# Expert tiles without gaps: 96 slots an expert instead of 128, in a two-block hybrid model on one core

## The chip, the cores and the metric

The kernel runs on one core of a Trainium2 chip. The metric is the device time of one execution in microseconds (us), and the lower the better. A core has TensorE (PE in the profile: matmuls, with its weight loads listed apart as PEld), VectorE (DVE), ScalarE (ACT), GpSimd (POOL) and SyncE (SP, which only issues transfers). Matmul results land in PSUM, of which a core has eight banks of 128 x 512 floats; everything else on the chip lies in SBUF.

## The reference, cut to what matters

1,024 tokens of 256 floats pass through two blocks. Every line below is applied to a layer-normed x and added to x.

```
x += shift-mix(x)              # block 0: a linear recurrence over time
x += first_ffn(x)              # 8 experts 256 -> 256, the best one of each token
x += state_space(x)
x += first_ffn(x)
x += attention_a(x)            # block 1: 16 heads of 16, 4 key groups, causal
x += second_ffn(x)             # 32 experts 256 -> 96 -> 256, the best four of each token
x += attention_b(x)            # the same shape, with a slope per head
x += second_ffn(x)

first_ffn:  p = softmax(x @ wg);  e = argmax p;  p[e] * (x @ W[e].T + b[e])
second_ffn: p = softmax(x @ router); the best 4, rescaled to sum 1;
            sum over them of w[e] * (silu(x @ gate[e].T) * (x @ up[e].T)) @ down[e].T
```

All of it is float32. In the inputs of this case, an expert gets at most 88 of a group's 512 tokens in the first FFN and at most 91 of them in the second (counted in the reference).

## The kernel before

The tokens are cut into two groups of 512 (g = 0, 1), and each group into four tiles of 128 tokens. Every stage is written for one group as a set of small generators, "streams", each of which yields after every few instructions. The name of a stream says what it is: A0 and A1 are shift-mix, F and G the first FFN in its two places, S state space, a and b the two attentions, e and f the second FFN after each, the digit the group, and a last letter the step. A list written out in the code, `ORDER`, names the streams one by one, and `follow` advances them in that order; so the order of instructions on each engine is fixed by this list. A second list, `BANKS`, gives the PSUM bank of every PSUM tile in the order in which the tiles are asked for. Stages of the two groups are woven together: e0 (second FFN of group 0) with attention a of group 1, attention b of group 0 with e1, f0 with attention b of group 1. Only f1 stands alone at the end.

**An expert FFN** (`second_ffn`, line 984; `first_ffn`, line 374, in the same manner) works by slots. `route` (990) computes the four experts of each token and its rank within each of them; its slot is `CAP * expert + rank`, with `CAP` = 128 (line 30). `send` (1042) scatters the normed tokens to these rows of a table `sent` in HBM, 16 indirect transfers a group on POOL's queue. Then 16 pairs of experts follow, two tiles of 128 rows a pair:

- `fetch` (1070): 256 rows from `sent` into `xe`, on SP's queue
- `turn` (1076): four TensorE transposes of 128x128 into a bank (`px`), ScalarE copies them to `xT`
- `gate` (1089): for each of the two tiles, two products (256 deep, so two halves of 128, line 198) of the 128 turned rows with 192 columns of gate and up weights, into `pgu`; ScalarE's silu, VectorE's product
- `turn_back` (1103): two transposes `ph`, VectorE copies `hT`
- `down` (1113): for each tile one product, 96 deep, with 256 columns, into `py`; VectorE copies it to `ye`; SP writes 256 rows of `done`

`back` (1129) gathers the rows of `done` with 16 indirect transfers on POOL's queue, and `add` (1141) adds each, weighted, to x. The first FFN has 8 experts, so 4 pairs; its `work` (491) is one product of 256 columns a tile and half, and VectorE adds a bias that lies in SBUF for all partitions (loaded in one transfer, line 1301). If any expert of any group had more than `CAP` tokens, a branch at the end (line 1516) computes all anew without slots.

**An attention** (`attention`, 774) holds its heads in strips of 32 partitions: partition 32 s + d holds depth d (of 16, and 16 helper rows) of key group s. A group's four units of 128 queries (batch b, query tile qt) go through five steps. `peaks` (842) makes scores to find the largest of each row: the keys were expanded before (`kb`, lines 801 to 806: four copies of the keys, each zero outside one strip), so a product takes 64 partitions, and two of them, on partitions 0 to 63 and 64 to 127, fill two banks; VectorE reduces each bank (line 864). `below` (870) turns the negated maxima and adds them to the queries (`qm`). `weights` (883) makes the transposed scores with the maxima taken off, again two products of 64 partitions at a time in two banks, and ScalarE's exp brings them to SBUF (`pT`, line 901), with the diagonal cut on POOL (904). `products` (909) multiplies them by the values: four products whose results have 32 partitions each, side by side in one bank (line 915). `finish` (921) divides and projects.

A float32 matmul appears in the trace as two weight loads and two matmul records, one after the other; a transpose as one of each.

## Time and profile before

| | |
|---|---|
| median of 14 runs | 739.22 us (734.62 to 742.86) |
| the profiled execution | 741.2 us |
| its span in the profile | 739.4 us |
| mean granted TensorE clock | 0.928 of full speed |
| TensorE busy | 630.8 us (85%), 3168 matmul records |
| VectorE busy | 489.7 us (66%) |
| GpSimd busy | 285.5 us (39%) |
| ScalarE busy | 258.1 us (35%) |
| moved by transfers | 94.01 MB |

A line of a group, as the profile writes it, has the line number in the code, the engine, the operation, what it writes and reads (names of tiles), the tile's shape as partitions x elements, and how often it occurs. For TensorE, a shape such as 64\*128 tells the rows and columns of the array that the matmul uses: 64 deep, and 128 partitions of result. A line of a timeline has a start, the time from there to the end of the last of its instructions, and the instructions; as matmuls are pipelined, the distance from one start to the next tells more of what an instruction costs than its own duration. A busy share is a share of time in which at least one instruction of the engine was under way. A table of stretches gives, for each, its length, the busy us and the number of instructions of PE, PEld, DVE, ACT and POOL, then the clock that TensorE was granted, the share of the DMA engines and the GB/s.

### The profile page before, as it was taken

Reading aid. Unit: us, or ns where it says so; the run is one execution under the profiler, and the core shown is the slowest. Engines: PE = TensorE matmul, PEld = TensorE weight load, DVE = VectorE, ACT = ScalarE, POOL = GpSimd, SP = SyncE. Lnnn points to the kernel's source line nnn. Section 1 sums busy time; section 2 is a strip of 40 time slices with the busy share of each in tenths; the row PEclk is TensorE's granted clock in tenths of the full one; section 3 lists DMA queues with packets and bytes.
Section 4 is the critical chain, followed back from the end, with each engine's and each line's share of the span. In section 5 each row is a group of like instructions: output and inputs, shape, how many; then the busy total and the mean of one; then the engine's idle time right before and its main releaser. Section 6 shows DMA issues by size and latency. Waiting matters only on the chain. (4 is left out here: it accounts for less than half of the span.)

```text
span 739.4 us, 10048 instructions
## 1 busy us (share of the span) xinstructions
PE 630.8 (85%) x3168; PEld 428.6 (58%) x3168; DVE 489.7 (66%) x1507; ACT 258.1 (35%) x476; POOL 285.5 (39%) x333
## 2 busy tenths in 40 slices
PE   4765859799999699998899998999996999999820
PEld 2343645366668455444369998853454449999810
DVE  7988536798854667758738546678867747645542
ACT  3522214667452122532354222332431345232200
POOL 3016233433642622511840726306704640625334
PEclk9896969999969699999999999999997999999965
DMA  6702333500004723690233867313100123877733
GB/s 194 263 0 72 139 118 128 182 0 1 1 28 156 268 74 107 216 318 15 86 100 129 271 218 245 122 58 100 44 1 22 65 86 111 267 229 207 226 113 104
DMA packets 70827, 94.01 MB, mean 127 GB/s; under 512 B 6896, under 2 KB 60656, under 8 KB 70128
## 3 DMA queue, kind: packets, MB, share of 16 engines
q1 hardware_dynamic: 62944, 72.31, 30.2%
q0 software_dynamic: 7680, 20.98, 9.1%
q8 instruction: 27, 0.44, 0.3%
q14 instruction: 32, 0.26, 0.1%
q10 hardware_dynamic: 144, 0.01, 0.0%
HBM read 50.29 MB, written 42.99 MB: 126 GB/s over the span
## 5 line engine op out<-in xcount | busy, mean ns | idle before, releaser
L1134 POOL DMA_INDIRECT yb_f<-done,bk_f x64 | 64.9, 1014 | 77.1 <-issue 23.7
L198 PE MATMUL pgu_f<-gu,xT_f 128*128 128x192 f32 x512 | 94.4, 331 | 0.0
L198 PEld LDWEIGHTS pgu_f<-gu,xT_f 128*128 128x128 f32 x512 | 85.2, 193 | 2.4 <-ACT xT_f L1086 0.8
L1046 POOL DMA_INDIRECT sent<-xn_f,to_f x64 | 62.7, 980 | 60.5 <-DVE to_f L1034 19.3
L1118 PE MATMUL py_f<-dw,hT_f 96*128 96x256 f32 x256 | 65.2, 382 | 0.6 <-DVE hT_f L1110 0.5
L1122 DVE COPY ye_f<-py_f 128x512 f32<-128x512 f32 x64 | 43.7, 686 | 24.6 <-PE py_f L1118 11.3
L864 DVE CUSTOM_DVE_ANT_0 junk_b<-pS_b,tri 128x128 f32<-128x128 f32 (+1 forms) x128 | 45.7, 357 | 17.0 <-PE pS_b L851 10.0
L864 DVE CUSTOM_DVE_ANT_0 junk_a<-pS_a,tri 128x128 f32<-128x128 f32 (+1 forms) x128 | 45.7, 357 | 13.5 <-PE pS_a L851 6.6
L1086 ACT COPY xT_f<-px_f 128x512 f32<-128x512 f32 x64 | 36.8, 587 | 40.0 <-PE px_f L1082 37.8
L1118 PEld LDWEIGHTS py_f<-dw,hT_f 96*128 96x128 f32 x256 | 44.7, 190 | 6.5 <-DVE hT_f L1110 1.4
L1098 ACT ACTIVATE he_f<-pgu_f 128x192 f32<-128x192 f32 x64 | 21.1, 331 | 77.8 <-PE pgu_f L198 68.4
L1144 DVE SCALAR_TENSOR_TENSOR x<-yb_f,wt_f,x 128x256 f32<-128x256 f32 x64 | 31.8, 503 | 21.2 <-DMA yb_f<-done,bk_f 20.7
L904 POOL TENSOR_SCALAR_AFFINE_SELECT pT_b<-pT_b 128x512 f32<-128x512 f32 x32 | 20.7, 672 | 47.2 <-ACT pT_b L901 47.0
L1100 DVE TENSOR_TENSOR he_f<-he_f,pgu_f 128x192 f32<-128x192 f32 x64 | 21.9, 348 | 25.3 <-ACT he_f L1098 25.0
L901 ACT ACTIVATE pT_a<-pST_a 128x512 f32<-128x512 f32 x48 | 25.6, 605 | 36.6 <-PE pST_a L893 36.0
L1082 PE MATMUL px_f<-ident,xe_f 128*128 128x128 f32 x256 | 36.6, 274 | 2.1 <-DMA xe_f<-sent 2.1
L1110 DVE COPY hT_f<-ph_f 96x256 f32<-96x256 f32 x64 | 26.1, 415 | 18.1 <-PE ph_f L1107 17.4
L901 ACT ACTIVATE pT_b<-pST_b 128x512 f32<-128x512 f32 x48 | 25.6, 600 | 33.0 <-PE pST_b L893 32.3
L904 POOL TENSOR_SCALAR_AFFINE_SELECT pT_a<-pT_a 128x512 f32<-128x512 f32 x32 | 19.9, 646 | 44.5 <-ACT pT_a L901 44.5
L1082 PEld LDWEIGHTS px_f<-ident,xe_f 128*128 128x128 f32 x256 | 30.4, 141 | 6.2 <-DVE x L1144 2.2
L198 PE MATMUL py_f<-W,xT_f 128*128 128x256 f32 x128 | 33.5, 413 | 0.2 <-ACT xT_f L488 0.2
L602 DVE SCALAR_TENSOR_TENSOR cv<-pcv,cw,cv 128x506 f32<-128x506 f32 (+5 forms) x36 | 26.3, 737 | 6.5 <-ACT cv L597 5.9
(298 smaller groups left out, 1328.3 us busy)
## 6 DMA issues: line engine op xcount, KB each, us to landing
xe_f<-sent SPq DMA_DIRECT2D x64, 256.0 KB, 3.2
done<-ye_f SPq DMA_DIRECT2D x64, 256.0 KB, 2.7
sent<-nil SPq DMA_DIRECT2D x16, 512.0 KB, 6.3
xe_f<-fsent SPq DMA_DIRECT2D x16, 256.0 KB, 2.9
fdone<-ye_f SPq DMA_DIRECT2D x16, 256.0 KB, 2.2
gu<-in_L1f_gate SPq DMA_DIRECT2D x4, 768.0 KB, 16.6
gu<-in_L1f_up SPq DMA_DIRECT2D x4, 768.0 KB, 11.9
dw<-in_L1f_down SPq DMA_DIRECT2D x4, 768.0 KB, 17.5
```

The source lines that it names most:

```text
L198: nc.tensor.matmul(dst, w(c), rhs(c), start=(c == 0), stop=(c == n - 1))
L602: nc.vector.scalar_tensor_tensor(cv[:, :, sh:], pcv[:, :, :S - sh], cw[:m, j, k:k + 1], cv[:, :, sh:], ALU.mult, ALU.add)
L864: nc.vector.tensor_tensor_reduce(out=junk[:, :w], in0=both[r][:, at:at + w], in1=tri[:, S - w:], scale=1.0, scalar=NEG, op0=ALU.add, op1=A ...
L901: nc.scalar.activation(pT.rearrange("p c q -> p (c q)"), pS, AF.Exp)
L904: nc.gpsimd.affine_select(pT, pT, pattern=[[0, AG], [1, P]], compare_op=ALU.is_ge, fill=zero, base=0, channel_multiplier=-1)
L1046: nc.gpsimd.indirect_dma_start(out=sent_to[g][t * TOPK + j], out_offset=bass.IndirectOffsetOnAxis(ap=to[:, t, j:j + 1], axis=0), in_=xn[:, ...
L1082: nc.tensor.transpose(px[:, j * P:(j + 1) * P], xe[q][:, k, c * P:(c + 1) * P], ident)
L1086: nc.scalar.copy(xT[q].rearrange("p k c t -> p (k c t)"), px)
L1118: nc.tensor.matmul(py[:, k * D:(k + 1) * D], hT[q][:, k, :], dw[:, 2 * q + k, :], start=True, stop=True)
L1122: nc.vector.tensor_copy(ye.rearrange("p k d -> p (k d)"), py)
L1134: nc.gpsimd.indirect_dma_start(out=yb, out_offset=None, in_=done[g], in_offset=bass.IndirectOffsetOnAxis(ap=kept_["back"][:, t, j:j + 1], ...
L1144: nc.vector.scalar_tensor_tensor(x[g][:, t, :], due[t, j], kept_["wt"][:, t, j:j + 1], x[g][:, t, :], ALU.mult, ALU.add)
```

## The change

Three things change, and the two lists are written anew for them.

1. `CAP` is 96. The table of an FFN has 96 rows an expert, so 3,072 rows instead of 4,096 in the second FFN and 768 instead of 1,024 in the first, and these rows are still cut into tiles of 128: 12 pairs of tiles instead of 16, and 3 instead of 4. A tile now holds rows of two experts, and the products with weights are made for pieces of it: `pieces` cuts a tile at the borders between experts into pieces of 64 or 32 rows that start at a multiple of their size. The result of a piece goes to the piece's own partitions.
2. The bias of the first FFN lies in SBUF by slots instead of by experts, in 12 transfers instead of one; the branch at the end loads it again for itself.
3. The expanded keys `kb` are gone. `peaks` and `weights` use the keys in their own strips of 32 partitions, four products at a time, into four banks.

```diff
-CAP = 128
+CAP = 96
-ORDER = """
...
+ORDER = """
...
-BANKS = """
...
+BANKS = """
...
+    def pieces(i):
+        at = 0
+        while at < P:
+            e, used = divmod(i * P + at, CAP)
+            n = next(n for n in (P, P // 2, P // 4)
+                     if n <= min(CAP - used, P - at) and at % n == 0)
+            yield e, slice(at, at + n)
+            at += n
...
+        pairs = E0 * CAP // (2 * P)
...
                 for j in range(2):
-                    e = 2 * q + j
-                    project(py[:, j * D:(j + 1) * D], lambda c: xT[q][:, j, c, :],
-                            lambda c: W[:, c, e * D:(e + 1) * D])
+                    for e, at in pieces(2 * q + j):
+                        project(py[at, j * D:(j + 1) * D], lambda c: xT[q][:, j, c, at],
+                                lambda c: W[:, c, e * D:(e + 1) * D])
...
-            kb = kept_["kb"] = pools["act"].tile([P, AG, TG], F32, tag="kb", name=f"kb_{name}", bufs=1)
-            for c in range(AG):
...
                 for c0 in range(0, 4, per):
-                    both = [bank("sq", f"pS_{n_}_{c0}_{r}") for r in range(2)]
+                    four = [bank("sq", f"pS_{n_}_{c0}_{s}") for s in range(AG)]
                     for c in range(c0, c0 + per):
-                        for r in range(2):
-                            rows, at = slice(64 * r, 64 * r + 64), (c - c0) * 2 * w
+                        for s in range(AG):
+                            rows, at = slice(32 * s, 32 * s + 32), (c - c0) * w
                             nc.tensor.matmul(
-                                both[r][:, at:at + 2 * w].rearrange("p (s k) -> p s k", s=2),
-                                qT[rows, c, q0:q0 + P],
-                                kb[rows, 2 * r:2 * r + 2, b * S:b * S + w],
-                                start=True, stop=True)
+                                four[s][:, at:at + w], qT[rows, c, q0:q0 + P],
+                                kT[rows, b * S:b * S + w], start=True, stop=True)
...
-                    for s0 in range(2):
-                        pairs = [(s, bank("st", f"pST_{n_}_{kt}_{s}")) for s in (s0, s0 + 2)]
-                        for s, pS in pairs:
-                            rows = slice(64 * (s // 2), 64 * (s // 2) + 64)
-                            nc.tensor.matmul(pS, kb[rows, s, k0:k0 + P],
+                    four = [bank("st", f"pST_{n_}_{kt}_{s}") for s in range(AG)]
+                    for s, pS in enumerate(four):
+                        rows = slice(32 * s, 32 * s + 32)
+                        nc.tensor.matmul(pS, kT[rows, k0:k0 + P],
...
-        pairs = E1 // 2
+        pairs = E1 * CAP // (2 * P)
...
                 for k in range(2):
-                    project(pgu[:, k, :], lambda c: xT[q][:, k, c, :],
-                            lambda c: gu[:, c, :, 2 * q + k, :])
+                    for e, at in pieces(2 * q + k):
+                        project(pgu[at, k, :], lambda c: xT[q][:, k, c, at],
+                                lambda c: gu[:, c, :, e, :])
...
                 for k in range(2):
-                    nc.tensor.matmul(py[:, k * D:(k + 1) * D], hT[q][:, k, :],
-                                     dw[:, 2 * q + k, :], start=True, stop=True)
+                    for e, at in pieces(2 * q + k):
+                        nc.tensor.matmul(py[at, k * D:(k + 1) * D], hT[q][:, k, at],
+                                         dw[:, e, :], start=True, stop=True)
...
-            nc.sync.dma_start(
-                bias, a["L0f_b"].rearrange("e d -> (e d)").partition_broadcast(P))
+            for i in range(E0 * CAP // P):
+                for e in range(i * P // CAP, ((i + 1) * P - 1) // CAP + 1):
+                    lo, hi = max(e * CAP - i * P, 0), min((e + 1) * CAP - i * P, P)
+                    nc.sync.dma_start(
+                        bias[lo:hi, i, :], a["L0f_b"][e, :].partition_broadcast(hi - lo))
```

The pieces repeat every three tiles (four experts). By width, in the order of the products: 64, 32, 32; then 64, 64; then 32, 32, 64.

## The prediction

> **What bounds the kernel now.** I read first the shares of the whole span, then a table of stretches, then two stretches of TensorE's timeline. The chain of waits at the page's end covers only the last gathers and says nothing of the middle.
>
> ```profile
> span 739.4 us, 10048 instructions
> PE 630.8 (85%) x3168; PEld 428.6 (58%) x3168; DVE 489.7 (66%) x1507; ACT 258.1 (35%) x476; POOL 285.5 (39%) x333
> ```
>
> The stretches show where the 85% lie:
>
> ```profile
> 290.00:380.00 90.00, 82.66 (x435) 39.89 (x435) 61.86 (x276) 36.28 (x72) 43.68 (x55) 1.00 0.48 152
> 380.00:460.00 80.00, 77.54 (x487) 70.98 (x482) 44.69 (x123) 27.86 (x59) 30.41 (x31) 0.98 0.63 199
> 460.00:570.00 110.00, 101.47 (x511) 61.06 (x511) 84.51 (x314) 36.71 (x70) 42.09 (x46) 0.96 0.20 61
> 570.00:640.00 70.00, 68.61 (x396) 45.24 (x393) 44.34 (x173) 28.82 (x56) 29.00 (x35) 0.99 0.36 112
> 640.00:708.00 68.00, 64.52 (x396) 58.77 (x395) 37.39 (x91) 18.15 (x42) 25.30 (x26) 1.00 0.71 223
> 708.00:740.00 32.00, 0.00 (x0) 0.00 (x0) 9.96 (x21) 0.00 (x0) 15.95 (x16) 0.51 0.36 104
> ```
>
> From 290 to 708 TensorE works 92 to 98% of the time, and no other engine comes near. These are the stretches that the change touches, so I count TensorE's time. The last 32 us (POOL's 16 gathers and their adds) and the first 100 (61 us of TensorE, chains of other engines) are left as they are.
>
> **What a matmul record costs** is read from one start to the next.
>
> ```profile
> 396.37 1.47 PE L198 MATMUL pgu_f<-gu,xT_f 128*128 128x192 f32 x8
> 397.67 0.38 PE L1107 MATMUL ph_f<-ident,he_f 128*96 128x128 f32 x2
> 397.89 0.60 PE L1082 MATMUL px_f<-ident,xe_f 128*128 128x128 f32 x4
> 398.33 1.03 PE L1118 MATMUL py_f<-dw,hT_f 96*128 96x256 f32 x4
> 399.22 1.57 PE L198 MATMUL pgu_f<-gu,xT_f 128*128 128x192 f32 x8
> ```
>
> 1.30 us for 8 records of 192 columns are 0.163 each; a transpose costs 0.109, a record of 256 columns 0.216 (median distance), one of 512 columns 0.429. A product is two records. Now the same where the shape of the used array changes:
>
> ```profile
> 306.30 1.13 PE L851 MATMUL pS_a<-kb_a,qT_a 64*128 64x256 f32 x8
> 307.37 1.13 PE L198 MATMUL po_a<-woa,cT_a 128*128 128x256 f32 x4
> 308.33 0.60 PE L248 MATMUL pt_a<-ident,xn_a 128*128 128x128 f32 x4
> 308.86 1.07 PE L915 MATMUL pctx_a<-pT_a,vaug 128*32 128x512 f32 x8
> 309.86 1.98 PE L198 MATMUL pk_a<-xnT_a,wka 128*128 128x512 f32 x4
> 311.77 1.13 PE L893 MATMUL pST_a<-qm_a,kb_a 64*128 64x512 f32 x4
> ```
>
> Two things are to be seen. Strips run side by side: the 8 records of 512 columns in four 32-wide strips (L915) take 1.00 us, where one after another they would take 3.43; so does each pair of 64-deep strips. And a change of shape costs time: the four transposes at 308.33 would end their issue at 308.77, the strips start at 308.86, 0.09 later; pk takes 1.91 for records worth 1.72. I compared the changes of shape in the whole trace: for each of the eight kinds that occur, the median of this gap is 0.092 to 0.096 us, whichever two shapes it joins. The first weights then load uncovered: 0.105 us more for 128 columns, 0.053 for 64 (the conv's 64-wide products: 0.481 to the second record, 0.429 after), 0.027 for 32. So a change costs 0.20 into full width or row strips, 0.15 into 64-wide, 0.12 into 32-wide columns.
>
> **Part by part, TensorE's time.** Two pieces of one width that follow each other lie in different strips: I call them one run. Three pairs of tiles (8 experts) have nine runs: 64 | 32 32 | 64 64, then 32 32 | 64 64 | 32 32, then 64 64 | 32 32 | 64. Neighbouring runs differ in width, so I take them as one after another, and the pieces of a run as side by side, as in L915.
>
> - `gate`: a piece is four records, a run 0.652 us. 48 pairs x 3 runs = 144 runs, 93.9 us; before, 64 pairs x 8 records = 83.5. **+10.4**
> - `down`: a run is 2 x 0.216. 144 runs, 62.2; before 256 records, 55.3. **+6.9**
> - the first FFN's `work`: a run is 4 x 0.216. 36 runs, 31.1; before 128 records, 27.6. **+3.5**
> - transposes: 16 pairs fewer x 6, and 4 pairs fewer x 4, at 0.109. **-12.2**
> - scores: `peaks` had 48 groups of two strips, each 0.86 us (two records of 512 or four of 256 deep in each strip); it has 24 groups of four strips, each again 0.86. `weights` likewise 48 to 24. **-41.2**. Four row strips aren't in the trace; two are (at full rate) and four column strips are. If four ran no faster than two, nothing of the 41 would be gained.
> - changes of shape, counted in the order of the built program: before 140 (112 into full width or row strips, 4 into 64-wide, 24 into 32-wide), 25.9 us; after 492 (153, 173, 166), 76.5. **+50.6**. 240 of the 492 lie between 64- and 32-wide pieces, the rest mostly around each pair's pieces, which transposes enclose.
>
> The sum is **+18.0 us**. [...]
>
> **Where the rows leave room.** (1) In `gate` and `work` the second piece stands behind four records of the first (each with its weight load). In the trace (pST groups that follow each other) a weight load passes at most three held instructions of the other strip; here it must pass five. If it can't, the second piece starts one record late: 7 of 9 runs, 16 x 7 x 0.163 + 4 x 7 x 0.216 = +24.3. `down` has two records a piece, the pattern of L915. Nearest is the rows' full overlap, so I take 0 and keep 24. [...] (2) A score group needs four free banks instead of two. Each is freed by an exp (0.60 us) or by reductions (0.29 to 0.42 each); a wait of one exp in each of 48 groups is +29, none if other products stand before it, as they do in the list; I take 0. (3) SP gets 12 bias transfers instead of one, at some 0.45 us of issue each, eight of them between the second and third fetch of F0. That is up to 4 us, in a stretch that TensorE doesn't fill; three pairs instead of four save about as much. I take 0.
>
> **Beside it, at nothing.** VectorE loses 16 x (348+415+686) ns, 4 x 0.69 and 8 x 0.484 (kb): 30 us. ScalarE loses 16 x (587+331) ns, 4 x 0.586 and 8 x 0.711: 23 us. About 13 of 94 MB aren't moved. TensorE covers all that, except where VectorE is nearly as full: 340 to 360 (17.2 of 20 us) and 500 to 540. There the shorter scores leave VectorE's reductions, unchanged in number, as the next bound, and TensorE gains only as far as the list has expert products to put there: both signs, some 10 us. TensorE's own idle time between 100 and 708 is 39 us, so a better list can't give more than that.
>
> **Rivals.**
> - *No drain between 64 and 32 wide*: then a tile's two or three pieces run side by side. gate takes 62.6, down 41.5, work 20.7: 41.6 less than before instead of 20.8 more; and 240 changes cost nothing, -32.4. Sum -76.8, so 662; with the late second piece 686. For it: strips work on their own, as L915 shows. Against: every pair of shapes in the trace drains. It decides the sign once a quarter of it holds (18 of 95).
> - *Pieces one after another*: 16 x 7 x (0.652+0.432) + 4 x 7 x 0.864 = +146, so 903. Against it is L915.
> - *Late second piece*: 781.
> - *The branch at the end is taken*: at most 91 tokens stand against 96 slots, so no. Its second FFN's products alone would add 32 x 4 x (8 x 0.429 + 8 x 0.216) = 660 us.
>
> **How the numbers follow.** The profiled execution took 741.2 us, 1.8 beyond its span and 2.0 above the median of 739.2. +18.0 gives 759.2 in its terms and **757** against the median. Chances: full overlap with drains 0.47 (own range 735 to 782), late second piece 0.26, no drain 0.15, one after another 0.05, and 0.07 for waits for banks or VectorE beyond the rest. The range of 80% goes from 686 (no drain, late piece) to 800 (late piece and part of the bank waits). Faster by over 0.3% (what a measurement can tell from no change): 0.15, a sixth of the first case, and little else: 0.25. Within it 0.05, slower 0.70.
>
> **What would show it.** In the profile after: gaps of 0.09 us and an uncovered load at each border of 64- and 32-wide records; a run of two gate pieces in 0.65 us (0.82 if late, 1.30 if one after another); score groups of 0.86 us plus a change; the stretch of f1, alone at the end, longer by some 17 us (4.3 for the runs; a quarter of the second FFN's 213 changes between widths at 0.135, and 24 blocks of pieces entered at 0.14 and left at 0.20, so 15.4; -2.6 for transposes). If 64- and 32-wide records start within 0.02 us of each other, the first rival holds. If VectorE passes TensorE where scores are made, the sum of TensorE alone was the wrong one.

## The result, and the profile after

The changed kernel takes **804.75 us** (median of 10 runs, 801.12 to 810.02) where the kernel before takes 739.88 (47 runs): 1.0893 times as long, interval 1.0863 to 1.0922. The sign was forecast, the size not: 757 with a range to 800. The profiled execution took 805.87 us. Its page, first the span and the first engine line:

```profile
span 804.2 us, 11830 instructions
...
PE 682.5 (85%) x4208; PEld 376.6 (47%) x4208; DVE 459.6 (57%) x1446; ACT 232.7 (29%) x429; POOL 281.0 (35%) x333
```

TensorE is busy for 52 us more with a third more records; VectorE lost the 30 us that were forecast, ScalarE 25. By busy time alone this looks like the kernel before, only longer. It isn't: where the scores are made there is less for TensorE to stream than before, and it takes longer. Here are 43 us among the scores of the first attention, in the table of stretches, before and then after (the columns from the second on: length, then busy us and instructions of TensorE, weight loads, VectorE, ScalarE and POOL, then the granted clock):

```profile
328.00:352.00 24.00, 19.47 (x115) 10.76 (x111) 20.42 (x91) 5.06 (x10) 4.00 (x6) 1.00 0.25 79
352.00:371.00 19.00, 16.37 (x91) 7.50 (x91) 14.35 (x74) 7.49 (x15) 15.43 (x18) 1.00 0.26 91
```

```profile
328.00:352.00 24.00, 16.57 (x85) 11.83 (x83) 15.03 (x62) 3.92 (x8) 3.63 (x5) 0.60 0.15 46
352.00:371.00 19.00, 19.00 (x75) 9.76 (x75) 13.62 (x59) 4.28 (x8) 11.06 (x12) 0.50 0.17 70
```

In the second row of after TensorE is busy for all of 19 us, with 75 records, at half clock; before, it ran 91 records in the same time and had time to spare. A busy share of 100% is here the sign of a slow clock, not of much work.

To say where the 65 us are I cut the main part into four stretches and each stretch into three kinds of time, worked out from the records of the two traces: a record streams its columns at the rate of 512 in 0.429 us, twice as long where the granted clock is half (in e16_clock, below, 46 records take 19 us at full clock and 47 take 39 us at half); records side by side count once. "Streaming" is this time at full clock, "half clock" what the slow clock adds to it, "nothing" the rest, in which TensorE streams no column (changes of shape, loads that nothing covers, waits). Scores 1 runs from the first score to the first gate product, e to e1's last gate product, scores 2 to f0's first, f to f1's last.

| us, before -> after | length | streaming | half clock | nothing |
|---|---|---|---|---|
| scores 1 | 117.6 -> 131.1 | 93.0 -> 78.8 | 0 -> 16.5 | 24.5 -> 35.8 |
| scores 2 | 115.7 -> 130.4 | 85.2 -> 81.7 | 2.7 -> 12.3 | 27.8 -> 36.4 |
| e | 108.6 -> 121.2 | 98.8 -> 91.3 | 1.7 -> 2.6 | 8.1 -> 27.3 |
| f | 96.0 -> 120.7 | 88.8 -> 91.7 | 0 -> 2.7 | 7.2 -> 26.3 |

So there are two losses. The stretches of expert products take 37 us more, nearly all of it "nothing": 312 changes of shape more (4 -> 157 and 0 -> 159) for 38.3 us, 0.12 each. The score stretches take 28 us more, though TensorE streams 18 us less there: 26 us of half clock and 20 us of "nothing" were added. The second loss is the one that was not forecast.

One border moved between the two kernels, and it shifts the shares. Before, 36 records of attention b's first queries, keys and scores (16 of 512 columns, 4 of 512, 16 of 256 in pairs of strips: 10.3 us of streaming at the rate above) stand ahead of e1's last gate product, so in row e; after, they stand behind it, in row scores 2. Like for like the expert stretches lost some 48 us and the score stretches some 18, in which TensorE streams 28 us less.

What TensorE waits for in the first score stretch, in the view of waits (total us, times, longest), before and then after:

```profile
PE pST_a L893 <- DVE qm_a L878: 3.5, 3, 2.3
PE pr_f L1013 <- DVE up_f L1008: 1.8, 1, 1.8
PE pm_a L874 <- DVE nmx L864: 1.2, 2, 0.9
PE po_a L198 <- ACT cT_a L946: 0.5, 1, 0.5
PE pcT_a L942 <- DVE cx_a L935: 0.3, 1, 0.3
```

```profile
PE pr_f L1005 <- DVE up_f L1000: 3.6, 1, 3.6
PE pcT_a L934 <- DVE cx_a L927: 2.2, 1, 2.2
PE po_a L190 <- ACT cT_a L938: 2.1, 3, 1.1
PE pST_a L885 <- DVE qm_a L872: 1.6, 2, 0.9
```

These are chains: scores, maxima on VectorE, turned maxima, queries less maxima, scores again, exp, context, division. TensorE waits longer for `up`, `cx` and `cT` than before, and less for `qm`; all waits of this view together grow from 7.7 to 15.2 us. That TensorE, with less work of its own between the links, comes to them earlier and stands there is a reading of these lines; the experiments test it.

### The profile page after: what moved, and what is told of

The parts are those of the page before. It is cut to its first block, busy times and chain, and to the rows that moved or that the text cites. A ratio compares the mean times of both kernels' runs of the same rounds, so it can differ in the third digit from the quotient of the medians.

```text
span 804.2 us, 11830 instructions
## 1 busy us (share of the span) xinstructions
PE 682.5 (85%) x4208; PEld 376.6 (47%) x4208; DVE 459.6 (57%) x1446; ACT 232.7 (29%) x429; POOL 281.0 (35%) x333
## 5 line engine op out<-in xcount | busy, mean ns | idle before, releaser
L190 PE MATMUL pgu_f<-gu,xT_f 128*32 128x192 f32 (+1 forms) x1024 | 120.7, 342 | 1.2 <-ACT xT_f L1075 1.1
L190 PEld LDWEIGHTS pgu_f<-gu,xT_f 128*32 128x32 f32 (+1 forms) x1024 | 66.7, 125 | 48.1 <-issue 36.1
L1109 PE MATMUL py_f<-dw,hT_f 96*64 96x256 f32 (+1 forms) x512 | 87.0, 402 | 2.6 <-DVE hT_f L1100 2.6
L1113 DVE COPY ye_f<-py_f 128x512 f32<-128x512 f32 x48 | 33.1, 689 | 59.0 <-PE py_f L1109 59.0
L1109 PEld LDWEIGHTS py_f<-dw,hT_f 96*64 96x64 f32 (+1 forms) x512 | 25.4, 122 | 51.9 <-issue 49.5
L1135 DVE SCALAR_TENSOR_TENSOR x<-yb_f,wt_f,x 128x256 f32<-128x256 f32 x64 | 32.2, 512 | 24.0 <-DMA yb_f<-done,bk_f 23.3
L190 PE MATMUL py_f<-W,xT_f 128*64 128x256 f32 (+1 forms) x256 | 41.6, 425 | 0.7 <-ACT xT_f L494 0.7
L1075 ACT COPY xT_f<-px_f 128x512 f32<-128x512 f32 x48 | 27.4, 586 | 50.6 <-PE px_f L1071 44.5
L893 ACT ACTIVATE pT_a<-pST_a 128x512 f32<-128x512 f32 x48 | 25.8, 601 | 33.5 <-PE pST_a L885 25.9
L1100 DVE COPY hT_f<-ph_f 96x256 f32<-96x256 f32 x48 | 19.8, 415 | 21.3 <-PE ph_f L1097 21.3
L1071 PE MATMUL px_f<-ident,xe_f 128*128 128x128 f32 x192 | 28.4, 284 | 2.6 <-DMA xe_f<-sent 2.6
L185 POOL TENSOR_TENSOR rstd_f<-var_f,neghalf 128x4 f32<-128x4 f32 x8 | 8.6, 1081 | 57.2 <-DVE var_f L224 57.2
```

What stands on the lines that cost most here:

```text
L190: nc.tensor.matmul(dst, w(c), rhs(c), start=(c == 0), stop=(c == n - 1))
L893: nc.scalar.activation(pT.rearrange("p c q -> p (c q)"), pS, AF.Exp)
L1071: nc.tensor.transpose(px[:, j * P:(j + 1) * P], xe[q][:, k, c * P:(c + 1) * P], ident)
L1075: nc.scalar.copy(xT[q].rearrange("p k c t -> p (k c t)"), px)
L1109: nc.tensor.matmul(py[at, k * D:(k + 1) * D], hT[q][:, k, at], dw[:, e, :], start=True, stop=True)
L1113: nc.vector.tensor_copy(ye.rearrange("p k d -> p (k d)"), py)
```

## The experiments

On some chips of this study the kernel before takes 784 to 796 us and not some 740, so each kernel is set against the kernel before on its own chip, and stretches are compared only among chips of one kind. The first four and the 13th to 15th, 17th and 18th, by the numbers in their names, ran on chips of the slower kind.

In the expectations, theory A: in the score stretches the chains of other engines set the end, so TensorE's saving buys little there. Theory B: TensorE's sum counts everywhere. Theory C, formed later: the half clock is a cause by itself; from then on A is written A', with the half clock as something that only goes with the waits. For the kernels on the usual chips, lengths of the stretches in us:

| kernel | median | ratio to before (interval) | scores 1 | e | scores 2 | f |
|---|---|---|---|---|---|---|
| before | 739.88 | 1 | 117.6 | 108.6 | 115.7 | 96.0 |
| e5_after | 806.15 | 1.0945 (1.0883 to 1.1007) | 126.7 | 120.5 | 130.3 | 120.9 |
| e6_twice | 829.27 | 1.1243 (1.1202 to 1.1285) | 141.1 | 121.3 | 144.3 | 120.6 |
| e7_whole | | | 128.0 | 84.3 | 127.1 | 82.7 |
| e8_bywidth | 776.82 | 1.0526 (1.0489 to 1.0564) | 128.8 | 109.1 | 129.4 | 109.4 |
| e9_fill | 802.62 | 1.0802 (1.0744 to 1.0860) | 128.5 | 120.2 | 128.6 | 121.0 |
| e10_bywidth_fill | 771.67 | 1.0407 (1.0357 to 1.0457) | 126.0 | 109.1 | 127.9 | 106.6 |
| e11_oldlist_bywidth | 768.83 | 1.0372 (1.0328 to 1.0416) | 120.8 | 106.7 | 130.0 | 105.1 |
| e12_oldlist_narrow2 | 733.09 | 0.9880 (0.9847 to 0.9913) | 118.3 | 93.3 | 126.8 | 88.4 |
| e16_clock | | | 117.7 | 120.3 | 133.0 | 120.7 |

### What the pieces cost: e7_whole, e8_bywidth

> The changed kernel itself, unaltered, beside the kernel before on this chip, as the measure for the others of this call. Both theories: ratio 1.089 to the kernel before (804.75 to 739.88). If the ratio is another on another chip, the others are compared with this run alone.

The control, alike within half a per cent.

```
-            n = next(n for n in (P, P // 2, P // 4)
-                     if n <= min(CAP - used, P - at) and at % n == 0)
+            n = P                                     # e7_whole
```

> The changed kernel with one product on the full tile in place of its two or three pieces (the weights of the tile's first expert for all 128 rows, so the FFN of the rows of the other experts is left out). By the rows: gate 93.9 to 62.6, down 62.2 to 41.5, the first FFN's products 31.1 to 20.7, changes of shape 492 to 112 (76.5 to 20.3 us): 118.6 less. Both theories: some 119 below e5_after, so 0.928 of the kernel before where e5_after is 1.089. Against the kernel before TensorE has then 101 us less to do by the same rows; theory B read from that side gives 640 of 740, theory A 686, as the scores' saving buys nothing. If it stays above 0.96 of the kernel before, the pieces aren't what the change lost.

Its whole time, 2383 us, can't be used: the branch at the end was taken, since the rows of the other experts feed the later router. Its main part can: the expert stretches fall from 241 to 167 us, the score stretches stay (255 against 257). TensorE has 101 us less to do than in the kernel before, by the rows (a few of them in first FFNs that lie ahead of the four stretches), and the four stretches together take 422 us against 438. Without any pieces at all, then, the change would have brought some 16 of these 101 us: of the loss, the pieces explain what lies in e and f and nothing of what lies among the scores.

```
+    def by_width(q):
+        two = [(k, e, at) for k in range(2) for e, at in pieces(2 * q + k)]
+        return sorted(two, key=lambda p: p[2].start - p[2].stop)
-                for k in range(2):
-                    for e, at in pieces(2 * q + k):
+                for k, e, at in by_width(q):          # e8_bywidth, in gate, down and work
```

> The changed kernel with the pieces of each pair of tiles in order of width, the 64-wide ones first: changes of shape 492 to 396 (13.4 us by their prices), runs 9 to 8 in three pairs (16 x (0.652 + 0.432) + 4 x 0.864 = 20.8 us). Both theories, since these lie where TensorE sets the end: up to 34 below e5_after, 25 to 34 if a part of the pieces lies beside the scores. If it is less than 15 below, the changes between widths are not what the pieces cost.

29.3 us below e5_after, 23 of them in e and f. The prices of the prediction (a change 0.12 to 0.20, a run 0.43 to 0.86) foretold 34. They hold.

### What the shorter scores bring: e6_twice and e2_pairs

```
-                    for c in range(c0, c0 + per):
+                    for c in 2 * list(range(c0, c0 + per)):      # peaks; likewise in weights
```

> The changed kernel with every score product of the attention issued twice into the same bank (the second writes the same numbers over the first): 48 groups more of 0.86 us on four strips, 41.2 us of TensorE, nothing else. This is just what the 32-row strips were to save. Theory B (TensorE's sum sets the end everywhere): 41 us above e5_after. Theory A (where the scores are made VectorE's reductions and the chains of other engines set the end, and TensorE waits, half of the time at half clock): 0 to 12 us above it, perhaps below it if the added work keeps the clock up.

23.1 us above, between the theories. In the score stretches streaming rises by 43.0 us, half clock falls by 6.4 and "nothing" by 8.0. So a us of TensorE added to the scores costs about half a us of the whole (28 us in the two profiles' score stretches): both theories had half of it. What a us taken away brings need not be the same, as the next run shows.

```
-                                kT[rows, b * S:b * S + w], start=True, stop=True)
+                                kb[rows, s, b * S:b * S + w], start=True, stop=True)
```

(with `kb` expanded as in the kernel before, `rows` 64 deep, the strips in order 0, 2, 1, 3; list and banks of the changed kernel)

> The changed kernel with one edit: scores are made again from expanded keys, 64 deep and two at a time, but in the same four banks and the same places of the lists; the expert pieces stay. It gives 41 us of TensorE time back to the scores (48 groups' worth in 24 places), and 8 expansions each on VectorE (0.48) and ScalarE (0.71). Theory A: TensorE waits in those stretches anyway, so at most +10 on 804.8, and fewer us at half clock than the 98 of the changed kernel. Theory B (TensorE's sum everywhere): +41, 846.

It ran on a chip of the slower kind: 867.59 us, 1.0963 (1.0894 to 1.1033) of the kernel before there. The changed kernel itself was not run on that chip; the nearest to it are e14_fill2 and e15_lightmax (below), 866.44 and 862.42 on that chip at another time. Beside e15_lightmax (whose reductions of one attention are lighter) it streams 33.5 us more in the score stretches, has 13.8 us less of half clock and 8.1 us less of "nothing". Strips of 32 rows instead of 64 thus buy at most some 5 us of the 41 in the new list (by the medians; the ratios, 1.0963 against 1.0955 and 1.0982, show no difference), and bring nearly half of the half clock with them.

### Is it the half clock or the waits: e9_fill, e10_bywidth_fill, e14_fill2

Products that nobody reads, in banks that were already held, where TensorE was seen waiting (three or four for `cx`, one to three for `qm`, one for `nmx`, 14 and 8 small ones for `up`):

```
+FILL = {("pcT", "a1_0_1_0"): 4, ("pcT", "b1_0_1_1"): 3, ("pST", "b1_0_0_0"): 3, ...}
+    def fill(to, times, rhs):
+        for _ in range(times):
+            nc.tensor.matmul(to, ident, rhs, start=True, stop=True)
```

> The changed kernel with products that nobody reads, put where TensorE stands waiting in the score stretches of the changed kernel's trace (waits of 0.8 to 3.6 us for qm, nmx, cx and up, found at the same places in three profiles): some 15 us of TensorE work in ten places, each in a bank that is already its own, and no longer than the wait there. Theory C (the clock halves after a stretch of 3.4 us in which TensorE streams less than some 0.4 of the time, and comes back only after one with over 0.8, so that a lighter score stretch runs its products at half speed): half clock in the two score stretches from 62 to 82 us down to under 25, and 15 to 30 us below the changed kernel (ratio 1.05 to 1.075 to the kernel before where the changed one is 1.0945). Theory A' (the waits set the end, the half clock only goes with them): within 5 us of the changed kernel. Theory B (TensorE's sum): 15 above.

The score stretches take 257.1 us, as in e5_after (257.0): streaming 161.3 -> 177.0, half clock 21.0 -> 18.0, "nothing" 74.5 -> 62.3. In the timeline of e9_fill (start, busy us, line, records, wait):

```profile
598.91 2.05 PE L266 MATMUL pr_f<-ident 128*128 128x128 f32 x16
602.24 0.49 PE L1018 MATMUL pr_f<-up_f,every 128*128 128x128 f32 x2 [1.28 <-DVE up_f L1012]
```

TensorE spends 2.05 us on products for nothing and still waits 1.28 for VectorE's `up` after them. The work cost nothing, as theory A' has it; but half clock hardly fell, so theory C was not really put to the test. The median is 3.5 us below that of e5_after (1.3% by ratio, on another chip), of which the profiled stretches show nothing; but the profiled run of e5_after was its fastest, 801.51.

> The same added products in the kernel with the pieces in order of width (which was 29 us below the changed one). The two act in different stretches, so theory C: 776.8 less 15 to 30, so 747 to 762, 1.01 to 1.03 of the kernel before. Theory A': 772 to 782.

771.67 us, 1.0407: below e8_bywidth by 1.1% by ratio, but above what theory C asked for (1.01 to 1.03). Both kernels with added products are thus some 1% below their partners, with intervals apart, and here the score stretches are shorter too (253.9 against 258.2). The added work cost nothing and may have gained a little; as the partners ran on another chip, that stays open.

```
+        ("pl", "f10_0"): 2, ("pl", "f11_0"): 2, ("pS", "a1_1_1_1"): 1, ...     # e14_fill2, on e9_fill
```

> The kernel with added products in TensorE's waits, and 8 us more of them where the first one's clock still fell: beside the router's logits of e0 and f0 (records of 32 columns, which stream little) and ahead of the two score groups of the third unit in a1, b0 and b1. Theory C (the half clock is a cause by itself): the extra time at half clock in the score stretches from 18 to under 8 us, and the two stretches together from 257 to 250 or less. Theory A' (chains of VectorE and ScalarE through the four banks set these stretches): 256 to 265, with less half clock and more streaming in the same time.

On a chip of the slower kind: 866.44 us, 1.0982 (1.0906 to 1.1058). The second score stretch of e15_lightmax, which ran beside it, is the one of the changed kernel, so it is the measure: 149.5 us there, 150.1 here, with 15.2 us more streaming, 8.5 less half clock, 6.1 less "nothing". Here the half clock did fall by a third, and the time stayed. That speaks against the half clock as a cause by itself, though the added products ate as much as it gave.

### Is it VectorE: e15_lightmax, e16_clock, e18_before_light

```
-                                out=junk[:, :w], in0=four[s][:, at:at + w],
+                                out=junk[:, :8], in0=four[s][:, at:at + 8],     # attention a only
```

> The changed kernel in which the reductions of the first attention layer's scores (128 instructions of 0.29 and 0.42 us) read 8 columns instead of 128 or 256 (the maximum that steadies the softmax is taken over the first 8 keys alone). VectorE loses some 25 to 30 us, all of it in the first score stretch. The second attention layer is unchanged and is the measure. Theory A' (VectorE frees the banks and its chain sets the end): the first score stretch from 127 to 131 us down to 112 to 120, the second as it was. Theory C or B: the first stretch within 4 us of what it was.

862.42 us, 1.0955 (1.0877 to 1.1034), on a chip of the slower kind, and the first score stretch at 131.3 us. In its first score stretch ScalarE waits once for 13.5 us, which the profile puts down to "remote"; no profile of the usual chips has such a wait, and it can have eaten the saving. So it was repeated on another chip, together with a test of the clock:

> The kernel with the lighter reductions of the first attention layer, and after its last product eight blocks on TensorE alone, back to back, each of 24 products of 512 columns (0.86 us each at full clock) on strips of these rows and columns: 128x128, 32x128, 64x128, 128x32, 64x128, four of 32x128 side by side, 32x128, four of 32x128. Its time is longer by the blocks and says nothing; read are the clock in each block and the two score stretches. Rows theory (shares of 0.37 and 0.77 of rows in use): full, half after one or two stretches of 3.4 us, half (0.5 isn't enough to return), back to full, full (0.5 is enough to stay), full, half, full. By rows times columns the fourth block would stay at half; by time in streaming alone all would be at full clock. The first score stretch, as before: 112 to 120 us if VectorE's reductions set it, 127 to 131 if not, the second 130.

The first score stretch takes 117.7 us instead of 126.7 and 131.1, the second 133.0: as theory A' expected. The groups of reductions, first in the changed kernel, then here (busy us, mean ns):

```profile
L858 DVE CUSTOM_DVE_ANT_0 junk_a<-pS_a,tri 128x256 f32<-128x256 f32 x64 | 27.1, 423 | 7.0 <-PE pS_a L848 3.5
L858 DVE CUSTOM_DVE_ANT_0 junk_a<-pS_a,tri 128x128 f32<-128x128 f32 x64 | 18.6, 291 | 18.1 <-PE pS_a L848 15.2 <-PE pm_a L868 0.5
```

```profile
L863 DVE CUSTOM_DVE_ANT_0 junk_a<-pS_a,tri 128x8 f32<-128x8 f32 x128 | 21.2, 165 | 27.0 <-PE pS_a L853 21.3
```

24.5 us less of VectorE, which is 57% busy over the whole span, took 9 to 13 us off this stretch. An engine with time to spare on the mean was on the path here. By the accounting of the first section the half clock is part of this gain: it adds 4.7 us here, 9.2 in e5_after and 16.5 in after, and "nothing" falls by 3 to 5 us. So the run shows what VectorE's reductions are worth, but does not part the waits from the clock.

The eight blocks of products, one row of the table of stretches for each once its clock had settled (the second block's first 4 us stand in a row by themselves):

```profile
764.00:782.00 18.00, 18.00 (x43) 7.98 (x42) 6.33 (x14) 0.00 (x0) 12.01 (x13) 1.00 0.41 119
783.00:787.00 4.00, 4.00 (x10) 1.67 (x10) 1.45 (x3) 0.00 (x0) 3.00 (x3) 1.00 0.49 126
788.00:818.00 30.00, 30.00 (x37) 11.61 (x36) 0.71 (x2) 0.00 (x0) 0.00 (x0) 0.50 0.02 6
820.00:859.00 39.00, 39.00 (x47) 15.06 (x47) 0.00 (x0) 0.00 (x0) 0.00 (x0) 0.50 0.00 0
867.00:883.00 16.00, 16.00 (x39) 4.07 (x38) 0.00 (x0) 0.00 (x0) 0.00 (x0) 1.00 0.00 0
885.00:904.00 19.00, 19.00 (x46) 8.32 (x45) 0.00 (x0) 0.00 (x0) 0.00 (x0) 1.00 0.00 0
905.00:925.00 20.00, 20.00 (x188) 9.48 (x188) 0.00 (x0) 0.00 (x0) 0.00 (x0) 1.00 0.01 2
931.00:964.00 33.00, 33.00 (x55) 13.31 (x57) 0.00 (x0) 0.00 (x0) 0.00 (x0) 0.50 0.00 0
966.00:986.00 20.00, 17.77 (x162) 9.76 (x154) 0.00 (x0) 0.00 (x0) 0.00 (x0) 1.00 0.01 3
```

TensorE is busy for the whole of each row (the last one reaches past the last product), and the clock is: full on 128 rows; half on 32 rows but for their first 4 us; half on 64 rows; full again on 128 rows, though only 32 columns wide; full on 64 rows, this time entered at full clock; full on four strips of 32 rows side by side; half on one strip; full on four. All eight as the count by rows said. On a strip of 32 rows that runs alone the granted clock is 0.50, as low as in the last 32 us of before, in which TensorE runs nothing (0.51).

The same reduction in the kernel before:

> The kernel before, in which the reductions of the first attention layer's scores read 8 columns (the maximum that steadies the softmax is taken over the first 8 keys alone). VectorE loses some 25 us in the first score stretch, which took 117.6 us. If VectorE came to set this stretch only with the shorter scores in groups of four banks: within 3 us of 117.6, and the whole within 0.5% of the kernel before. If it set it already: 108 to 112 us, and 6 to 9 us in the whole.

789.58 us, 0.9995 (0.9957 to 1.0033), on a chip of the slower kind, where e15_lightmax had shown nothing either. Whether VectorE set the first score stretch before the change too stays open.

### Old list, and pieces of one width: e1, e3, e4, e11, e12, e13, e17

e3_oldlist is the kernel before with the changed FFNs; in the list every fourth pair's place yields and does nothing. e4 and e1 cut all pieces 32 wide (`n = P // 4`) in the old and the new list. All three ran, like e2_pairs, on one chip of the slower kind, where the kernel before takes 788.31.

> The kernel before with the expert FFNs alone changed to 96 slots and pieces of 64 and 32; its scores, its order and its banks stay (of each four pairs of tiles in the order the fourth is left empty). TensorE's sum: runs +20.8, transposes -12.2, changes of shape 140 to 524, 25.9 to 82.7, so +65.4 and 805. Theory A: 800 to 810, the time of the changed kernel, because the four-strip scores and the new order together gave nothing. If the pieces cost less than their rows say and the new order is the loss: 760 or less.

843.83 us, 1.0699 (1.0638 to 1.0760): the FFN part alone is slower by itself, as its changes of shape say (the sum had asked for 65 us, 55.5 came).

Beside it e2_pairs parts the shorter scores from their list. Both cut the same pieces and make scores 64 deep, but e2_pairs does so in the new list, in groups of four banks: 867.59 us against 843.83, 1.0963 against 1.0699, with intervals apart. In the two profiles the score stretches of e2_pairs take 23.4 us more: 16 of "nothing", 5 of half clock, 2 of streaming (the expert stretches take 11 us more; the profiled run of e2_pairs was its slowest, that of e3_oldlist its fastest). At equal score products, then, the new list with its groups of four banks costs some 24 us on this chip, by the medians. Which of the two does, the order or the groups, was not parted.

> As the one before, but with every piece 32 wide. TensorE's sum against the kernel before: runs -41.6, transposes -12.2, changes of shape 140 to 286, 25.9 to 49.0, so -30.7: 709. Theory A: 705 to 725, as the score stretches are those of the kernel before. If pieces of 32 in four strips don't run side by side in gate and work, above 780.

795.83 us, its runs between 780.44 and 799.54: no difference from the kernel before that could be told there, where the sum had asked for 0.96.

> Old list and old 64-deep scores with both FFNs on 96 slots (every fourth pair's place in the list left empty), pieces in order of width: 98 changes of shape and 16 runs fewer than in the kernel of this kind before (13.7 + 20.8 us). Both theories: 29 to 34 below it in the same terms, so 1.025 to 1.035 of the kernel before, where it was 1.070. If the score stretches then take what they do in the kernel before (118 and 116 us), the loss in the changed kernel's score stretches comes with its scores and list, not with the pieces.

768.83 us on a usual chip, 1.0372, just above what was expected. The score stretches take 120.8 and 130.0 us, not the 118 and 116 that were asked for; but in the second stands work that moved in from row e, most of what moved in the changed kernel, and streaming in both together is up by 10 us. "Nothing" takes 52.8 us (before 52.3, changed kernel 72.2) and half clock 9.7 (2.7 and 28.8). The added waits, and most of the half clock, come with the new scores in groups of four banks and their list, not with the pieces.

Set beside e8_bywidth (1.0526), which cuts the same pieces in the same order, the old list with the old scores is 1.5% faster. The shorter scores in their new list, which were to save 41 us, cost some 11.

> Old list and old scores with both FFNs on 96 slots in pieces that are all 32 wide, a second time, since the first was on a chip where the kernel before takes 788 us and its own runs lay 2% apart. By TensorE's sum 0.96 of the kernel before; if TensorE's instructions come too slowly for pieces so short (waits that the profile puts down to issue, 18 us of them there), 0.99 to 1.01 as there.

**733.09 us, 0.988 of the kernel before (0.9847 to 0.9913): the only version that beats both**, by 1.2%. Its page:

```profile
PE 613.8 (84%) x4848; PEld 357.0 (49%) x4848; DVE 465.4 (64%) x1455; ACT 242.3 (33%) x440; POOL 284.9 (39%) x333
```

Pieces of 32 rows need more records (4848 against 3168), but four lie side by side, and no change lies between them: e and f take 181.7 us against 204.6 before. The sum had asked for 0.96, and what is missing isn't a wait for instructions: ScalarE, VectorE and TensorE together wait 1.8 us for "issue" here. The score stretches take 245.1 us against 233.3, most of it by the work that moved in.

> The changed kernel with one edit: every piece is 32 wide, so that a tile is four pieces side by side and no border between 64 and 32 wide is left; lists and all else as in the changed kernel. Theory A (pieces cost what their rows say; in the score stretches VectorE's reductions and chains of short steps set the end, so TensorE's saving there buys nothing and its clock halves while it waits): 96 us less TensorE time than the changed kernel (runs 187.2 to 124.8, changes of shape 492 to 252, 76.5 to 42.6), nearly all of it in stretches that TensorE fills: 710 to 730. Theory B (TensorE sets the end everywhere and the new order loses the 47 us): the same 96, 709. If the borders between widths were not the cost, the time stays near 800.

> The changed kernel with all pieces 32 wide, a second time, because the chip of its first run starved TensorE of instructions (40 us of waits put down to issue, the kernel before 788 us). With old list and old scores such pieces took the stretches of expert products to 182 us. If only these stretches differ, the two score stretches stay at 255 to 262 and the whole falls by 60: 741 to 752 us where the changed kernel takes 805, 1.00 to 1.02 of the kernel before. By the sum of the rows it would be 709.

> The changed kernel with all pieces 32 wide, on a chip where the kernel before takes some 740 us. The stretches of expert products from 242 to 182 us, as with such pieces in the old list, the two score stretches at 255 to 262: 741 to 752 us, 1.00 to 1.02 of the kernel before. By the sum of the rows it would be 709, 0.96.

All three met chips of the slower kind: 807.27, 810.35 and 811.00 us, 1.0261, 1.0266 and 1.0234 of the kernel before (the first from 1.0174 to 1.0348, the others like it). The price on a usual chip was not measured. In the expert stretches half clock takes 17 to 21 us there and "nothing" 62 to 66, where e12_oldlist_narrow2 on a usual chip has 6 and 36; that took much of what the pieces gave. TensorE's waits for "issue" come to 24.6 us in the profile of e1_narrow (40 stands in the expectation of e13_narrow2); what held the instructions back was not shown.

## Why the prediction was wrong

The step that failed is "**scores ... -41.2**", and with it "Room (2)", the wait for four free banks, which was taken at 0, and the choice to add up TensorE's time alone in stretches that hold chains. Point by point, by the distances from one start to the next in the main part (first score to last gate product, +65.4 us):

- *Changes of shape, +50.6.* Right. The gap between 64- and 32-wide records is 0.095 to 0.097 us (0.092 to 0.096 was used), and the rival "no drain", in which this gap is missing between the two widths, is refuted: across such a border no two records of the second FFN start nearer than 0.255 us.
- *Runs of 0.652 in `gate`, 0.432 in `down`, 0.864 in `work`, pieces side by side.* Right. A gate run and the change behind it take 0.781 us (32 wide) and 0.808 (64 wide), forecast 0.77 and 0.80; a `down` run 0.556 to 0.583. The second piece starts 0.013 us after the first, so "late second piece" and "one after another" are both refuted.
- *The FFN terms together* (gate +10.4, down +6.9, first FFN +3.5, transposes -12.2, changes +50.6: +59.2): 54.5 measured in `pgu`, `py`, `px` and `ph`.
- *f1 alone at the end, +17.* From its first gate product to its last 7.5 us (45.6 to 53.1); 24.7 for f0 and f1 together. A block has 80 changes more, not 101; entering and leaving pieces had been counted besides changes that they replace.
- *Scores -41.2.* 12.4: `pS` and `pST` went from 107.7 to 95.3 us. Four row strips do run at full rate side by side (8 records of 512 columns in 1.14 us in e5_after), so the shape was right. What failed is that a group needs its four banks at once. Before, 44 of the 48 groups of `weights` (`pST`) have all their records started within 0.54 us of the first; after, of 24 groups only eight do so within 0.58, three more take 1.03 at half clock, and the others up to 3.27. Together the 24 take 17 us more than if all had started in 0.55. In the timeline of after the banks come one by one:

```profile
359.42 2.58 PE L848 MATMUL pS_a<-kT_a,qT_a 32*128 32x256 f32 x15
361.38 1.61 PE L885 MATMUL pST_a<-qm_a,kT_a 32*128 32x512 f32 x2
361.80 0.63 PE L848 MATMUL pS_a<-kT_a,qT_a 32*128 32x256 f32 x1
362.24 3.48 PE L885 MATMUL pST_a<-qm_a,kT_a 32*128 32x512 f32 x6
```

The first two records of this group start at 361.38, the other six 0.9 us later, and all eight last until 365.7: 4.3 us for 0.86 us of work, a factor of two of it the clock. What holds the last strips stands in the rows of the weight loads, which wait with them:

```profile
362.71 0.50 PEld L885 LDWEIGHTS pST_a<-qm_a,kT_a 32*128 32x128 f32 x2 [0.44 <-DVE nmx L858]
363.64 0.50 PEld L885 LDWEIGHTS pST_a<-qm_a,kT_a 32*128 32x128 f32 x2 [0.44 <-DVE nmx L858]
```

Each strip is let go by a reduction of VectorE (`nmx`), and two of these, 0.42 us each, lie between one strip and the next, 0.93 us. The queries and keys of all four strips are there by then, as the first strip runs on them; so what is waited for is the bank, which holds scores that aren't reduced yet. "Room (2)" named such a wait, priced it at +29 (one exp in each of 48 groups), and took 0 because other products stand before it in the list. That the 29 lie near the 28.8 missed here is luck: part of these is half clock. Between 363.4 and 366.8 TensorE streams for 88% of the time, but with 38% of its rows, and from 366.9 on for 96% with 58%; the clock stays at half until 373.7.
- *Everything else, 0.* +23.3 us, in products that the change doesn't touch: the context's +7.2, the turned context +3.9, the logits +3.6, the turned maxima +2.8. They run at half clock, or they are charged with the wait ahead of them. In e11_oldlist_bywidth they take what they took before (context 30.0 against 29.8, turned context 8.4 and 8.3, logits 7.7 and 7.4, turned maxima 18.2 and 18.2), so this loss too comes with the new scores and their list.
- *"VectorE ... as the next bound ... some 10 us".* The place was right: 340 to 360 was named, and the clock falls at 333 in after. The size was not, and the clock was not thought of. The sign that was named, VectorE passing TensorE where scores are made, hardly came: in stretches of 20 us of after it does so once, from 560 to 580, by 17.38 to 17.25 us. It doesn't have to, as e16_clock shows.
- *Two readings.* The first 100 us hold 62.2 us of TensorE (61 is the first 92), and the first FFN's products of F, which the sum counts, lie there from 77 us on. The first rival decides the sign from a fifth of it on (18 of 95), not a quarter. Neither moves the result.

So 47.4 us of error are 28.8 from the scores, 23.3 from work around them, and -4.7 from the FFNs. Shown: the pieces' cost (e7, e8); that score products that are added count only half (e6); that the new list with its groups of four banks costs some 24 us at equal scores, on a chip of the slower kind (e2 beside e3), and that together with the shorter scores it loses some 11 us on the usual ones (e8 beside e11); that VectorE's reductions are worth 9 to 13 us in the first stretch (e16); that in eight blocks of products the clock followed the rows in use (e16). Only argued: how the loss of the score stretches divides between chain, banks and clock. The clock falls where TensorE waits (in after at 332.7, behind 3.41 us in which it streams for 34% of the time), and the slow clock then lengthens the links that TensorE has in the chains; no run parted the two. Not tried: the new scores in the old list.

## What to carry to other kernels

Count the time of an engine as gain only in stretches where it is the one that waits for nobody; where chains through other engines run, double the suspected work first and see how much of it shows, and take what shows as the most that a saving can bring (here half showed, and hardly any of the saving came). Products on strips of unequal width paid some 0.12 to 0.16 us at each border here, so cut all pieces to one width, even if they are more. Let strips of few rows start together: a strip that waits for its bank leaves the others on fewer rows, and in e16_clock the clock was 0.50 on one strip of 32 rows and 1.00 on four side by side.

## What the runs showed of the hardware

**The granted clock followed the rows in use.** In the traces of before and after it is 1.00 or 0.50, and each time at one of the two lasts 3.41 us or a whole multiple of it, up to 194.56 us (but for the last of each trace, 33.0 and 33.1). Cut into pieces of 3.41 us, these two traces have 358 pieces at full clock: where rows in use times time was under 0.37 of all rows, half clock followed, and above it full, but for 2. From half clock, in 82 pieces, full followed after 0.77 or more and not after less, without exception. The two bounds were fitted to traces of this case; by time in streaming alone, rows left out of account, the best bounds miss 3 of the 358 and 6 of the 82. e16_clock tested them on new patterns, but only with shares of a quarter, a half and all of the rows: at a half the clock stayed at 1.00 in one block and at 0.50 in the other, whichever it was entered at. With TensorE busy for all of 33 us on one strip of 32 rows it was 0.50: there the half clock came without idle time.

**Chips differ, in waits that the profile puts down to "issue" and "remote".** On the slower kind the kernel before takes 784 to 796 us. In the profile of e18_before_light, whose instructions on VectorE and ScalarE have the mean durations of before within 0.5% in 14 of the 16 groups that the two lists by form share (the other two are 2 and 10% shorter), there are waits that the usual chips' profile of before doesn't have (times and longest as above):

```profile
ACT he_f L1099 <- remote: 39.1, 6, 10.6
DVE he_f L1101 <- issue: 17.6, 8, 8.2
PE ph_f L1108 <- issue: 9.7, 2, 6.1
```

In all, ScalarE waits 96.8 us for "issue" and "remote" there, VectorE 38.8 and TensorE 15.6; in the profile of before these are 1.5, 0 and 0.2. What holds the instructions back was not looked into.
